# The last block of an attention-and-convolution kernel worked in two parts, with three small reorderings before it

## The chip, the cores and the metric

The kernel runs on one core of a Trainium2 chip. The time is that of the device in microseconds (us), for one execution of the whole program; the median over several executions is compared. The engines are TensorE (PE, with its weight loads as PEld), VectorE (DVE), ScalarE (ACT), GpSimd (POOL) and SyncE (SP); SP, ACT and POOL also issue transfers (DMA).

## The reference

Two layers act on x of shape 8 x 64 x 64 x 64 (batch, channels, height, width), all in four-byte floats. The first is attention over the 4096 pixels of an image, with the means of queries and keys taken off, and a unary term:

```python
sim = softmax(einsum('bcn,bcm->bnm', q - q_mean, k - k_mean) / 8, axis=2)
out = einsum('bnm,bcm->bcn', sim, v) + out_unary[:, :, None]
x = x + out.reshape(b, C, h, w)
```

The second takes the signs of the result, convolves them with signed weights of 1x1, 3x3 and 5x5 taps, scales each and adds the three, and gates the sum by the image's mean:

```python
s = qconv_bn(x, w1) + qconv_bn(x, w3) + qconv_bn(x, w5)   # binact(x) = sign(x), bin_weight(w)
gate = sigmoid(grouped(mean(s, axis=(2, 3)), gw) + gb)     # then a channel shuffle
return s * gate[:, :, None, None] + x
```

`bin_weight` takes the sign of each weight less its output channel's mean, times the mean of the absolute values. The gate needs the whole image's s, so nothing of an image can be stored before its last row of s is there.

## The kernel before, in words

Two images share the 128 partitions: a pair. There are four pairs. A pair's 4096 queries are worked in eight blocks of `QB` = 512, so there are 32 blocks, numbered g from 0 to 31. A block is a loop of `NK` = 32 steps over tiles of 128 keys. In a step, `scores` (L493) makes four 64x64 matmuls, one in each quadrant of the array, into a score bank `ps` and ScalarE takes the exponential of 128x1024 into a tile `e` (a pool of five buffers, L508); `weighted` (L511) makes four matmuls from the previous step's `e` into two accumulators `acc` (L516); `summed` (L524) lets VectorE add `e` to a running sum `es` (L534). Four-byte matmuls are recorded as two instructions each. In all blocks but the last, four of the 32 tiles are added in DRAM by transfers instead (`DRAM_TILES`).

What else has to be done is hung onto the steps by `plan(g)` (L1092): `put(i, f)` calls f after step i's matmuls were issued. This list alone sets the order on every engine; there is no scheduler behind it. At step 0 of block g, `weighted_out` (L536) copies the two accumulators of block g−1 to SBUF, the first by ScalarE (L541), the second by VectorE (L542), then `mix_rows` (L990) makes the queries of block g+1 and the convolutions of block g−3, as products of combined rows: `products(k, names)` of the 5x5 and the 3x3. Those of the 3x3 go to the two banks of the accumulators (0 to 3 to the first, 4 and 5 to the second). `hold` (L827) takes a product out scaled, by ScalarE, and `join` (L836) adds another on VectorE. In the steps that follow, the sums of block g−1 come back (`fold_first`, `fold`, `fold_last`, `spread`), the values are tested for 0 and infinity (`check_block`), and `added`, `finish`, `signs_wide` and `signs` make x and its signs.

In block 1, `mean_rows_out` (L219) makes the weights' means by one product (`nmb_p`, L221) and a copy, `centre` (L226) takes them from the weights on VectorE, and `weight_signs` (L232) takes the signs on ScalarE (L233), for the 5x5, the 3x3 and the 1x1 at steps 3 to 10.

In the last block (g = 31) there is no next block. `mix` (L939) makes the plain convolutions of block 29 at step 22 and of the first six rows of the joint blocks 30 and 31 at step 27; a 5x5 or 3x3 tap is one matmul (L891), and `convs_out` (L899) adds the three results on VectorE (L915). After the loop, block 31 is finished: accumulators out in parts of 320 and 192 columns, sums by a matmul with ones (`sums_wide`, L598), reciprocals in pieces of 128 (L609), `added`, `finish`, signs, copies of signs to the other half of the partitions by VectorE and GpSimd, then `mix` for rows 6 to 10 and 11 to 15, the test, `gate_mean` and `gate` (L919 to L932), and the stores: two blocks by a product with the gate on a diagonal (L1261) and ScalarE, six by VectorE (L936) and SyncE (L937).

Of the kernel before, what the change touches and what calls it, by code (L numbers as in the profile page):

```python
# [40 lines left out]
DRAM_TILES = (5, 11, 17, 23)  # L41
LOW, HIGH = 1e-20, 1e20
# [3 lines left out]
def conv_seq_kernel(ctx, tc, x, wq, wk, wv, vecs, w1, w3, w5, wtap, gw, out):  # L46
# [72 lines left out]
    fit = cp.tile([P, 2, n_pairs * (NQ + 1)], F32, tag="fit", name="fit")  # L119
# [157 lines left out]
    class Pair:  # L277
# [3 lines left out]
        def __init__(self, name, xt):  # L281
            self.name, self.x = name, xt
            self.xs = sm.tile([P, 8], F32, tag="xs", name=f"xs_{name}")
            self.q, self.x2, self.s, self.y1, self.acc = {}, {}, {}, {}, {}
            self.es, self.r, self.joint, self.sc, self.gap, self.t = {}, {}, None, None, None, None
# [147 lines left out]
        def check(self, r, i, sides=(0, 1)):  # L433

            w = r.shape[-1]
            for side in sides:
                if w < QB:
                    junk = self.tile(sm, "ck", f"{i}_{side}", (P, 8), BF16)
                else:
                    junk = self.tile(fp, "rc", f"ck_{i}_{side}", dtype=BF16)  # L440
                nc.scalar.activation(  # L441
                    junk[:, 0:w],
                    r,
                    AF.Sign,
                    bias=lim[:, side : side + 1],
                    scale=1.0 - 2.0 * side,
                    accum_out=fit[:, side, i : i + 1],
                )
# [44 lines left out]
        def scores(self, qb, j, neg=None):  # L493
            ps = ps_s.tile([P, 2, QB], F32, tag="s", name=f"ps_{self.name}_{qb}_{j}")
            for h in range(2):
                for b in range(2):
                    nc.tensor.matmul(  # L497
                        ps[img[h], b, :],
                        self.x[img[b], bass.ds(j * P + h * H, H)],
                        self.q[qb][img[b], :],  # L500
                        start=True,
                        stop=neg is None,
                    )
# [3 lines left out]
            e = ep.tile([P, 2, QB], F32, tag="e", name=f"e_{self.name}_{qb}_{j}")  # L507
            nc.scalar.activation(e, ps, AF.Exp, scale=1.0 / 8.0)  # L508
            return e

        def weighted(self, qb, j, e):  # L511
            if j == 0:
                self.acc[qb] = acc_banks(f"acc_{self.name}_{qb}")
            for b in range(2):
                for h in range(2):
                    nc.tensor.matmul(  # L516
                        self.acc[qb][h][img[b], :],
                        self.v[img[h], j, img[b]],
                        e[img[h], b, :],
                        start=(j == 0),  # L520
                        stop=(j == NK - 1),
                    )

        def summed(self, qb, j, e, dram=False):  # L524
# [5 lines left out]
            elif j == 1:  # L530
                self.es[qb] = self.tile(sm, "es", qb, (P, 2, QB))
# [4 lines left out]
        def weighted_out(self, qb, parts=(slice(0, QB),)):  # L536

            acc = self.acc[qb]
            self.acc[qb] = [self.tile(fp, f"o{h}", qb) for h in range(2)]
            for c in parts:  # L540
                nc.scalar.copy(self.acc[qb][0][:, c], acc[0][:, c])  # L541
                nc.vector.tensor_copy(self.acc[qb][1][:, c], acc[1][:, c])  # L542
# [55 lines left out]
        def sums_wide(self, qb):  # L598
            self.sums_p = m_tile(f"su_{self.name}_{qb}")
            es = self.es.pop(qb)  # L600
            for b in range(2):
                nc.tensor.matmul(self.sums_p[img[b], :], ones[:, 0:C], es[:, b, :], start=True, stop=True)  # L602

        def reciprocals_wide(self, qb, cols):
            if cols.start == 0:
                self.r[qb] = self.tile(fp, "r", qb)
            for a in range(cols.start, cols.stop, P):
                c = slice(a, min(a + P, cols.stop))
                nc.vector.reciprocal(self.r[qb][:, c], self.sums_p[:, c])  # L609

        def added(self, qb, cols=slice(0, QB)):
            if cols.start == 0:
                self.x2[qb] = self.tile(bp, "x2", qb)
            acc = self.acc[qb]
            nc.vector.tensor_tensor(self.x2[qb][:, cols], acc[0][:, cols], acc[1][:, cols], ALU.add)
# [211 lines left out]
        def hold(self, z, i, n, by):  # L827
# [6 lines left out]
            nc.scalar.activation(out, z, AF.Identity, scale=frac[:, by : by + 1])  # L834
# [64 lines left out]
        def convs_out(self, rows, z, n):  # L899
# [10 lines left out]
            if n == 0:  # L910
                nc.scalar.activation(s, z[0][0][:, 0:w], AF.Identity, bias=shift, scale=scale[:, 0:1])
                return
            for h in range(len(z[n])):
                gap = dict(accum_out=self.gap_column()) if (n, h) == (2, 1) else {}
                nc.vector.scalar_tensor_tensor(  # L915
                    s, z[n][h][:, 0:w], scale[:, n : n + 1], s, ALU.mult, ALU.add, **gap
                )

        def gate_mean(self):  # L919
            self.ga = self.tile(sm, "ga", 0, (P, 1))  # L920
            nc.vector.tensor_reduce(self.ga, self.gap[:, 0 : self.n_gaps], AX.X, ALU.add)

        def gate(self):
            pg = m_tile(f"pg_{self.name}")
            for b in range(2):
                nc.tensor.matmul(
                    pg[img[b], 0:1], gw_s[img[b], img[b]], self.ga[img[b]], start=True, stop=True
                )
            self.gt = self.tile(sm, "gt", 0, (P, 1))
            nc.scalar.activation(self.gt, pg[:, 0:1], AF.Exp, bias=ngb, scale=-1.0 / N)  # L930
# [8 lines left out]
    def mix(q, c, one=None, two=None):  # L939
# [47 lines left out]
        if c is not None:  # L987
            p.convs_out(rows, z, 2)

    def mix_rows(q, c):  # L990
# [6 lines left out]
        if c is not None:  # L997
# [6 lines left out]
            seqs[0] += products(5, 4, 5) + products(3, 4, 5, 0, 1, 2, 3) + [((1,), 0, 1.0)]  # L1004
# [13 lines left out]
        for _, h, b, (n, i, _) in order:  # L1018
# [27 lines left out]
            elif n == (3, 5):  # L1046
                p.hold(acc[1][:, 0 : 4 * HH], 6, 2, 0)
# [34 lines left out]
    def attend(pairs):  # L1082
# [9 lines left out]
        def plan(g):  # L1092
# [32 lines left out]
            if g == 1:  # L1125
                put(0, mean_rows_out)
# [9 lines left out]
            if g >= 1:  # L1136
# [6 lines left out]
                put(13, p.added, b)  # L1143
                put(15, p.finish, b)
                put(16, p.signs_wide, b, 2)
                put(18, p.signs_wide, b, 1)
                put(20, p.signs, b)
# [27 lines left out]
            if g == 1:  # L1175
                for i, n in enumerate((2, 1, 0)):
                    put(3 + 3 * i, centre, n)
                    put(4 + 3 * i, weight_signs, n)
# [27 lines left out]
            if g == n_blocks - 1:  # L1206
                put(1, pairs[-1].join_blocks)
                put(22, lambda: mix(None, rows(n_blocks - 3), one_bank, score_banks))
                put(27, lambda: mix(None, (pairs[-1], pairs[-1].joint_rows(0, 6)), one_bank, score_banks))
            return at  # L1210

        for g in range(n_blocks):
            pr, qb = divmod(g, NQ)
            at = plan(g)
            p = pairs[pr]
            for j in range(NK):
                new = (p, qb, j, p.scores(qb, j))
                if pending is not None:
                    pending[0].weighted(*pending[1:])
                    pending[0].summed(*pending[1:], g < n_blocks - 1)  # L1220
                for f, a in at.pop(j, ()):
# [3 lines left out]
        pending[0].weighted(*pending[1:])  # L1225
        pending[0].summed(*pending[1:])
# [3 lines left out]
        parts = [(0, 5), (5, ROWS)]  # L1230
        p.weighted_out(b, [slice(r0 * HH, r1 * HH) for r0, r1 in parts])
        p.sums_wide(b)

        pre = acc_banks("pre")
        for i in range(2):
            nc.tensor.matmul(pre[i], ident, p.x2[i], start=True, stop=False)
        warm(10)
        halves = [slice(r0 * HH, r1 * HH) for r0, r1 in parts]
        p.added(b, halves[0])
        p.reciprocals_wide(b, halves[0])  # L1240
        p.finish(b, halves[0])
        p.added(b, halves[1])
        p.reciprocals_wide(b, slice(halves[1].start, halves[1].start + P))
        for (r0, r1), cols in zip(parts, halves):
            if r0 > 0:
                p.reciprocals_wide(b, slice(cols.start + P, cols.stop))
                p.finish(b, cols)
            for n in (2, 1):
                p.signs_wide(b, n, r0, r1, None)
                p.copy_signs(b, n, r0, r1, (nc.vector.tensor_copy, nc.gpsimd.tensor_copy))  # L1250
            p.signs(b, r0, r1, nc.gpsimd.tensor_copy)
        mix(None, (p, p.joint_rows(6, 11)), one_bank, score_banks)
        mix(None, (p, p.joint_rows(11, 16)), one_bank, score_banks)
        p.check(p.r[b], n_blocks - 1)
        p.gate_mean()
        p.gate()
        diag_g = sm.tile([P, P], F32, tag="diag_g", bufs=1, name="diag_g")
        nc.vector.tensor_scalar(diag_g, ident, p.gt, None, ALU.mult)
        rows_p = rows_of(n_pairs - 1)
        for i in range(2):  # L1260
            nc.tensor.matmul(pre[i], diag_g, p.s[i], start=False, stop=True)  # L1261
            nc.scalar.copy(p.s[i], pre[i])
            nc.scalar.dma_start(out=of[rows_p, bass.ts(i, QB)], in_=p.s[i])
        for i in range(2, NQ):
            p.store(i, rows_p)

    with tc.manual_schedule():
# [21 lines left out]
        attend([first] + [None] * (n_pairs - 1))  # L1289


    nb_ = sm.tile([P, 1], F32, tag="nb", name="nb")
    nc.vector.tensor_reduce(nb_, fit, AX.XY, ALU.add)
    nc.vector.tensor_scalar(nb_, nb_, n_pairs * (16.0 * NQ + 2.0) - 16.0 + 2 * QB, None, ALU.is_equal)
    pb = m_tile("pb")
    nc.tensor.matmul(pb[:, 0:1], ones, nb_, start=True, stop=True)
    good = sm.tile([P, 1], I32, tag="good", name="good")
    nc.vector.tensor_copy(good, pb[:, 0:1])
# [121 lines left out]
```

## Time and profile before

| what | value |
|---|---|
| time, median of 3 | 1902.15 us (1902.07 to 1902.22) |
| the profiled execution: its own time | 1902.25 us |
| its span, first to last instruction | 1900.4 us |
| busy: TensorE, VectorE, ScalarE | 1881.3, 1587.7, 1276.6 us |
| granted TensorE clock, mean | 0.997 |
| one `e` of 128x1024: exponential, sum | 1025 ns, 1221 ns |
| last store issued, last one landed | 1893.1, 1897.9 us |

The busy shares come from matmuls whose ends are modelled, so TensorE's 99% says that it is seldom without work, not how well it is used. In a timeline row the first two numbers are start and length in us, then come engine, line, operation, output<-input, and in brackets the idle time before it and what ended it. In the chain of waits each row is a stretch of the chain that ended last: start, length, engine and line.

### The profile page before, as it was taken

To read this page: it belongs to the slowest core of one execution; us is meant where nothing else is said; L and a number is where in the kernel's file an instruction comes from. 1 tells how busy PE (TensorE), PEld (TensorE's weight loads), DVE (VectorE), ACT (ScalarE), POOL (GpSimd) and SP (SyncE) were. 2 spreads that over 40 slices of the span, in tenths; PEclk is the share of its full clock that TensorE was granted. 3 is DMA by queue.
4 is the path that set the end of the run, shared out by engine and by line. 5 is a ranking of instruction groups with operands and counts; after the bars stand their busy time and mean duration, and the time that the engine had idled before them with its cause. 6 is when DMAs were issued, how large, how long until landed. Compare 5 with 4: busy or idle time off the path is not lost.

```text
span 1900.4 us, 50311 instructions
## 1 busy us (share of the span) xinstructions
PE 1881.3 (99%) x21494; PEld 785.8 (41%) x21494; DVE 1587.7 (84%) x2485; ACT 1276.6 (67%) x1639; POOL 129.4 (7%) x177
## 2 busy tenths in 40 slices
PE   9999999999999999999999999999999999999997
PEld 4334344343344434444434444434433344444343
DVE  6888888889888888888888888888887888887876
ACT  5666776666666676666666667666666666666663
POOL 0000000000000000000000000000000000000000
PEclk9999999999999999999999999999999999999998
DMA  4334433333333533333333444333333344333311
GB/s 124 60 62 106 83 65 72 66 58 72 67 70 87 117 83 80 65 72 66 58 71 68 104 111 92 52 78 67 70 67 66 63 85 93 85 71 63 72 35 47
DMA packets 73025, 142.23 MB, mean 75 GB/s; under 512 B 10380, under 2 KB 40920, under 8 KB 72664
## 3 DMA queue, kind: packets, MB, share of 16 engines
q0 software_dynamic: 22352, 81.29, 24.1%
q1 hardware_dynamic: 49864, 56.53, 10.3%
q8 instruction: 170, 2.79, 0.6%
q10 hardware_dynamic: 576, 1.11, 0.2%
q14 instruction: 63, 0.52, 0.1%
HBM read 39.27 MB, written 89.78 MB: 68 GB/s over the span
## 4 chain that ended last, share of the span: by engine, by line
PE 90%; DVE 1%; DMA 0%; ACT 0%; issue 0%; ACTq 0%
PE ps L497 43%; PE acc L516 43%; PE z L804 2%; PE pq L483 1%; PE pv L336 1%; PE z L891 0%; PE z_5e L804 0%; DMA es<-e 0%; PE pre L1261 0%; DVE r L609 0%; ACT e L508 0%; ACT rc_ck L441 0%; DVE es L534 0%; PE su L602 0%; DVE es_j L915 0%
## 5 line engine op out<-in xcount | busy, mean ns | idle before, releaser
L508 ACT ACTIVATE e<-ps 128x1024 f32<-128x1024 f32 x1024 | 1049.0, 1025 | 571.9 <-PE ps L497 557.7
L534 DVE TENSOR_TENSOR es<-es,e 128x1024 f32<-128x1024 f32 x836 | 1020.5, 1221 | 192.4 <-ACT e L508 178.7
L497 PE MATMUL ps<-q,x 64*64 64x512 f32 x8192 | 1087.3, 590 | 1.5 <-ACT q L466 0.8
L516 PE MATMUL acc<-e,v 64*64 64x512 f32 x8192 | 1085.2, 589 | 0.6 <-ACT e L508 0.6
L516 PEld LDWEIGHTS acc<-e,v 64*64 64x64 f32 x8192 | 326.3, 131 | 554.8 <-ACT e L508 316.6
L497 PEld LDWEIGHTS ps<-q,x 64*64 64x64 f32 x8192 | 348.2, 133 | 489.8 <-issue 264.3
L555 POOL DMA_DIRECT2D es<-e x93 | 80.1, 862 | 900.3 <-ACT e L508 597.3
L871 DVE SCALAR_TENSOR_TENSOR sb<-pt,sb 128x256 f32<-128x256 f32 x174 | 65.8, 419 | 0.0
L804 PEld LDWEIGHTS <-wc 64*64 64x64 bf16 x3364 | 60.0, 106 | 2.7 <-issue 1.0
L555 POOL DMA_DIRECT2D es<-es x31 | 26.6, 859 | 440.2 <-DVE es L534 426.1
L532 DVE TENSOR_TENSOR es<-e,e 128x1024 f32<-128x1024 f32 x32 | 39.2, 1225 | 18.1 <-ACT e L508 18.1
L804 PE MATMUL z<-ec,wc 64*64 64x128 bf16 x1392 | 53.6, 217 | 0.0
L804 PE MATMUL z<-t,wc 64*64 64x128 bf16 x1392 | 53.1, 217 | 0.3 <-DVE o L542 0.3
L652 ACT ACTIVATE s<-x,vec 128x512 bf16<-128x512 f32 (+2 forms) x66 | 46.1, 702 | 5.6 <-DVE x L620 5.6
L834 ACT ACTIVATE pt<-z,frac 128x256 f32<-128x256 f32 (+1 forms) x87 | 41.1, 543 | 8.9 <-PE z L804 8.9
L839 DVE SCALAR_TENSOR_TENSOR pt<-z_5e,frac,pt 128x256 f32<-128x256 f32 x29 | 14.0, 484 | 38.2 <-PE z_5e L804 38.2
L553 POOL DMA_DIRECT2D es<-e x31 | 17.4, 561 | 340.2 <-ACT e L508 328.9
L542 DVE COPY o<-acc 128x512 f32<-128x512 f32 (+2 forms) x33 | 22.2, 675 | 9.6 <-PE acc L516 9.6
L845 DVE TENSOR_TENSOR pt<-pt 128x384 f32<-128x384 f32 x58 | 29.6, 552 | 0.0
L336 PEld LDWEIGHTS pv<-wx,x 64*64 64x64 f32 x1024 | 22.1, 134 | 16.6 <-issue 8.9
L570 DVE TENSOR_TENSOR e_parts<-e_parts 128x512 f32<-128x512 f32 x31 | 21.3, 687 | 7.3 <-DMA e_parts<-es 7.3
L620 DVE SCALAR_TENSOR_TENSOR x<-x,ou,x 128x512 f32<-128x512 f32 (+2 forms) x33 | 24.3, 736 | 1.2
(178 smaller groups left out, 880.5 us busy)
## 6 DMA issues: line engine op xcount, KB each, us to landing
es<-e POOLq DMA_DIRECT2D x124, 512.0 KB, 5.3
es<-es POOLq DMA_DIRECT2D x31, 512.0 KB, 5.4
e_parts<-es SPq DMA_DIRECT2D x124, 128.0 KB, 3.1
r<-rc SPq DMA_DIRECT2D x62, 128.0 KB, 2.8
out<-sb SPq DMA_DIRECT2D x28, 256.0 KB, 3.0
x<-in_x SPq DMA_DIRECT2D x24, 256.0 KB, 4.9
ec<-t SPq DMA_DIRECT2D x29, 99.0 KB, 4.8
xc<-in_x SPq DMA_DIRECT2D x30, 72.0 KB
```

What stands on the lines that cost most here:

```text
L336: nc.tensor.matmul(pv[img[h], b, i * w : (i + 1) * w], self.x[img[b], bass.ds((4 * g + i) * P + h * H, H)], self.wx[img[b], :], start=True ...
L497: nc.tensor.matmul(ps[img[h], b, :], self.x[img[b], bass.ds(j * P + h * H, H)], self.q[qb][img[b], :], start=True, stop=neg is None,)
L508: nc.scalar.activation(e, ps, AF.Exp, scale=1.0 / 8.0)
L516: nc.tensor.matmul(self.acc[qb][h][img[b], :], self.v[img[h], j, img[b]], e[img[h], b, :], start=(j == 0), stop=(j == NK - 1),)
L532: nc.vector.tensor_tensor(self.es[qb], self.first, e, ALU.add)
L534: nc.vector.tensor_tensor(self.es[qb], self.es[qb], e, ALU.add)
L555: nc.gpsimd.dma_start(out=out, in_=e, accum_op=ALU.add)
L652: nc.scalar.activation(sy[n][0][:, rows, pad : pad + HH], self.x2[qb][:, r0 * HH : r1 * HH].rearrange("p (h w) -> p h w", w=HH), AF.Sign, ...
L804: nc.tensor.matmul(z[img[b], :].rearrange("p (q w) -> p q w", w=HH), wc[k][img[h], n, c * C : c * C + C], src[:, first : first + step + 1 ...
L834: nc.scalar.activation(out, z, AF.Identity, scale=frac[:, by : by + 1])
L845: nc.vector.tensor_tensor(self.pairs[:, :, :, r, :], t[:, 0:3, 0], t[:, 0:3, 1], op)
L871: nc.vector.scalar_tensor_tensor(out, x, by, out, ALU.mult, ALU.add, **gap)
```

## The change

There are four parts.

In `mix_rows`, the products of the 3x3 come in the order 0, 4, 5, 1, 2, 3 instead of 4, 5, 0, 1, 2, 3, and product 5 is taken out of its bank by VectorE instead of ScalarE.

In block 1, `mean_rows_out` moves from step 0 to step 5, `centre` from steps 3, 6, 9 to 7, 10, 13, and `weight_signs` from 4, 7, 10 to 8, 11, 14.

The last block is worked in `PARTS`: 384 queries in 32 steps with one tile of 128 keys each, then 128 queries in eight steps with four tiles of keys each. The steps of its plan are scaled by 512/384 (`plan_last`), `added` to `signs` start two steps sooner, and all of the first part's finish (sums, reciprocals, signs and their copies by transfers, test) is hung onto the second part's steps.

After the loop only 128 queries are left to finish. The convolutions are cut at rows 6 to 11 and 12 to 15, with other banks; the mean covers all but the last rows, and the logits add the last two columns of sums by further matmuls (`gate_logits`); of the last rows, one 5x5 result is scaled by ScalarE and added late. The product with the gate's diagonal is kept for one block, the diagonal is made by ScalarE, and VectorE and SyncE store seven blocks. The final test for 0 and infinity moves into this stretch.

```diff
+PARTS = ((slice(0, 384), 1), (slice(384, QB), 4))
-        def scores(self, qb, j, neg=None):
+        def scores(self, qb, j, neg=None, part=(slice(0, QB), 1)):
+            cols, n = part
+            w = cols.stop - cols.start
...
+            for i in range(n):
+                for h in range(2):
+                    for b in range(2):
+                        nc.tensor.matmul(
+                            ps[img[h], b, i * w : (i + 1) * w],
+                            self.x[img[b], bass.ds((n * j + i) * P + h * H, H)],
+                            self.q[qb][img[b], cols],
...
+            for t in range(n * j, n * j + n):
+                at = (t - n * j) * w
+                for b in range(2):
+                    for h in range(2):
+                        nc.tensor.matmul(
+                            self.acc[qb][h][img[b], 0:w],
+                            self.v[img[h], t, img[b]],
+                            e[img[h], b, at : at + w],
...
+            if vector:
+                nc.vector.tensor_scalar(out, z, frac[:, by : by + 1], None, ALU.mult)
+            else:
+                nc.scalar.activation(out, z, AF.Identity, scale=frac[:, by : by + 1])
...
-            seqs[0] += products(5, 4, 5) + products(3, 4, 5, 0, 1, 2, 3) + [((1,), 0, 1.0)]
+            seqs[0] += products(5, 4, 5) + products(3, 0, 4, 5, 1, 2, 3) + [((1,), 0, 1.0)]
...
-                p.hold(acc[1][:, 0 : 4 * HH], 6, 2, 0)
+                p.hold(acc[1][:, 0 : 4 * HH], 6, 2, 0, True)
...
-                put(0, mean_rows_out)
+                put(5, mean_rows_out)
...
-                    put(3 + 3 * i, centre, n)
-                    put(4 + 3 * i, weight_signs, n)
+                    put(7 + 3 * i, centre, n)
+                    put(8 + 3 * i, weight_signs, n)
...
+        def plan_last():
+            at, (first, _) = {}, PARTS
+            for i, steps in plan(n_blocks - 1).items():
+                at[i * QB // first[0].stop] = steps
...
+            put(NK - 5, lambda: mix(None, rows(n_blocks - 3), one_bank, score_banks))
+            put(NK - 2, lambda: mix(None, (p, p.joint_rows(0, 6)), one_bank, score_banks))
+            put(NK, p.weighted_out, b, cols)
+            put(NK + 1, p.added, b, cols)
+            put(NK + 1, p.sums_wide, b, first)
+            put(NK + 1, p.reciprocals_wide, b, cols)
+            put(NK + 2, p.finish, b, cols)
+            put(NK + 3, lambda: p.check(p.r[b][:, cols], n_blocks - 1))
+            put(NK + 4, p.signs_wide, b, 2, 0, r1)
+            put(NK + 5, p.signs_wide, b, 1, 0, r1)
+            put(NK + 6, p.signs, b, 0, r1)
...
+        mix(None, (p, p.joint_rows(6, 12)), acc_bank(0), score_banks)
         p.gate_mean()
-        p.gate()
+        p.check(p.r[b][:, cols], n_pairs * (NQ + 1))
+        mix(None, (p, p.joint_rows(12, 16)), acc_bank(1), score_banks, True)
+        p.gate_logits()
...
+        nc.tensor.matmul(pre, ident, p.x2[0], start=True, stop=False)
+        p.gate_out()
+        nc.scalar.activation(diag_g, ident, AF.Identity, scale=p.gt)
+        nc.tensor.matmul(pre, diag_g, p.s[0], start=False, stop=True)
+        nc.scalar.copy(p.s[0], pre)
+        nc.scalar.dma_start(out=of[rows_p, bass.ts(0, QB)], in_=p.s[0])
+        p.store(1, rows_p)
...
         for i in range(2, NQ):
             p.store(i, rows_p)
```

## The prediction

> **What bounds the kernel now.** I read the page's busy shares first, then the chain of waits, then the timeline of four places: a block boundary, block 1, the value products, the end.
>
> ```profile
> PE 1881.3 (99%) x21494; PEld 785.8 (41%) x21494; DVE 1587.7 (84%) x2485; ACT 1276.6 (67%) x1639; POOL 129.4 (7%) x177
> PE 90%; DVE 1%; DMA 0%; ACT 0%; issue 0%; ACTq 0%
> ```
>
> TensorE sets the time. A step of the loop is `ps` 0.858 us, then `acc` 0.858 us, back to back; 32 steps make 54.9 us, 32 blocks 1758 us. Only a hole in TensorE, or the end, can be gained. At the boundary before block 30's second step:
>
> ```profile
> 1750.91 0.69 DVE L542 COPY o<-acc 128x512 f32<-128x512 f32 x1 [0.32 <-PE acc L516]
> 1750.94 0.58 ACT L541 COPY o<-acc 128x512 f32<-128x512 f32 x1
> ...
> 1751.53 0.22 PE L804 MATMUL z<-ec,wc 64*64 64x128 bf16 x1
> 1751.65 0.21 PE L804 MATMUL z<-t,wc 64*64 64x128 bf16 x1
> ```
>
> Products normally start 0.03 us apart at most here; this start comes 0.12 after the last, 0.05 after VectorE's copy has emptied the second accumulator at 1751.60: a hole of 0.09. ScalarE had emptied the first at 1751.52. Every boundary from block 3 to 30 shows the same. Block 1 has two larger holes:
>
> ```profile
> 76.60 0.44 DVE L490 TENSOR_SCALAR q<-pq,mx 128x224 f32<-128x224 f32 x1
> 77.10 0.59 PE L221 MATMUL nmb_p<-diag,ones 64*128 64x192 f32 x2 [1.37 <-DVE q L490]
> 85.76 1.54 ACT L233 ACTIVATE wt<-w_tap 128x1600 bf16<-128x1600 f32 x1
> 88.26 1.09 PE L516 MATMUL acc<-e,v 64*64 64x512 f32 x8 [0.28 <-ACT e L508]
> ```
>
> The weights' means wait for a bank that the queries hold, and all later matmuls wait behind them; then ScalarE's signs of 1600 columns make an exponential late (0.45 lost: `acc` was due at 87.81). The chain at the end, from the last exponential:
>
> ```profile
> 1869.85 1.03 ACT e L508
> 1870.91 1.24 DVE es L534
> 1872.19 1.10 PE su L602 x4
> 1873.32 2.19 DVE r L609 x3
> ...
> 1876.88 0.87 DVE r L609
> ...
> 1881.49 0.96 PE z L891 x16
> ...
> 1885.59 0.57 DVE es_j L915 x2
> ...
> 1887.38 0.17 DVE gt L932
> ```
>
> From TensorE's last `acc` (ends 1871.8) to the gate (1887.56) take 15.8 us, serial, with VectorE's reciprocals (0.73 per 128 columns), then signs, copies and two convolutions.
>
> **What the Trainium skill says.** "PSUM — Partial Sum Buffer", PSUM bank collisions raise a hardware error: guard PSUM by bank and quadrant, so a product may not enter an accumulator that is still being read; the hole of 0.09 is that. The same page, Engine vs sequencer instructions: ScalarE's and VectorE's queues are strict FIFO; the late exponential of block 1 agrees. "TensorE: Matmul & The Clock Gate", LDWEIGHTS: about P/1.2 ns for P columns, and Part 3, The mechanism: loads overlap only when the row group differs. That makes 53 ns per 64 columns and, two in turn, an estimate of 107 ns for four quadrants. The value products, four-byte with 65 moving columns, contradict it:
>
> ```profile
> 29.05 0.64 PE L336 MATMUL pv<-wx,x 64*64 64x65 f32 x32
> 29.51 1.09 PE L497 MATMUL ps<-q,x 64*64 64x512 f32 x8
> ```
>
> 32 matmuls with their loads pass in 0.46 us, 0.0575 per four. The trace decides.
>
> **3x3's products.** Product 0 needs the accumulator that ScalarE empties 0.07 to 0.08 sooner. Products 4 and 5 follow three columns (0.17) later, when VectorE is done. 29 boundaries by 0.07: −2.0 us; at least 0 (the hole reappears), at most 29 by 0.09, 2.6. The evacuation of product 5 moves from ScalarE (0.45, 256 columns) to VectorE (0.47, by L490's 0.44 for 224). VectorE is idle there 1.3 us before the join that waits for `z_5e`, so it costs nothing; uncovered, 0.47 by 29 is 13.6.
>
> **Block 1.** The means' product leaves step 0. Queries end at 75.54, `ps` runs to 76.4, `acc` waits for VectorE's copy (76.00 to 76.68), and step 2's `ps` begins at 77.60 instead of 79.38: −1.78. In step 5 the product costs its own 0.32. Then it gets worse: VectorE's queue from the means' copy is copy 0.36, fold 0.68, 0.42, 0.45, one sum 1.23, 0.41, 0.20, 0.45, centring 1.81, together 6.0 us with no room between. With TensorE's step 5 at 83.2 the copy begins at 85.64, centring ends at 91.6, the signs end at 93.2, the exponential queued behind them at 94.1, while `acc` is due at 93.05: a hole of 1.15 for the old 0.45. Sum −1.78 + 0.32 + 0.70 = −0.8; between −1.9 (no new hole) and +0.3.
>
> **The last block.** Columns are the same, so TensorE's products cost the same, if the loads, doubled to 512 recorded, hide: four per 0.107 us of 128-column passes, against 0.0575 shown. The steps of 384 last 1.288; the sum of 768 columns is 0.95 (between L615's 0.686 for 512 and L534's 1.221 for 1024), 1.02 with the dependence on the one before; the exponential about 0.80. VectorE's slack per microsecond falls from 1 − 1.29/1.717 = 25% to 1 − 1.02/1.288 = 21%; over the 20 us of joins, folds and pairs that is 0.8 us. What TensorE gets added:
>
> - sums of the first 384 columns inside the loop, 0.86 × 0.75 = 0.65;
> - sign of block 30 at step 18, queued on ScalarE behind VectorE's `finish`, which now sits 1 us behind its exponential: exponentials 19 and 20 slip, 1.0 (0 to 2.5);
> - short first step, waiting for the accumulators: 0.1;
> - after each convolution the second-next `ps` takes the bank that VectorE empties; a shorter step gives 0.43 less cover, twice: 0.85 (before: 0.42 and 0.13 lost);
> - the first 128-column `acc` behind both evacuations: 0.3;
> - the two checks of 384 (0.8 each) ahead of an exponential: 0.3.
>
> Together +3.2 (0.7 to 6): the last `acc` ends at 1875.0 on the old clock. From there, with the durations of 128 columns set a little under the rows of 192 (0.36, 0.42, signs 0.40): last sum 0.35, sums by TensorE 1.0, hand-over 0.3, one reciprocal of 128 0.73, two products 0.75, three signs 0.85, z0's evacuation 0.65: at +4.6 VectorE starts on the convolution. The convolution of rows 6 to 11 needs only the first part's signs and runs on TensorE meanwhile (2.8 us); rows 12 to 15 follow (1.87) and are done 0.8 before VectorE's end. GpSimd's copies of 128 columns (0.35 for 192 now) lie beside rows 6 to 11; uncovered they would cost 0.7. VectorE: three sums of 384 (0.62 each, 2.1 with gaps), mean 0.2, two of 256 (0.48, 0.57), to +7.95; logits 0.35, exponential 0.26, two small ones 0.31, latencies 0.45: gate at +9.3, not +15.8. The late addition (0.42) and the test of the limits (0.23, 0.15) that stand on VectorE before the gate's last steps fit beside logits and exponential (0.9 with hand-overs); without that cover they cost 0.8. So −6.4 + 3.2 = −3.2.
>
> After the gate VectorE stores seven blocks instead of six but no longer makes `diag_g` first; the last issue is at gate + 5.7 against 5.6, and the transfers' landing (1897.9, 10.3 after the gate) moves with it: 0 ± 0.8. SyncE issues one store more (0.36 to 0.6), in that count; its new part copies (four transfers of the first part) have 3 us before the convolution asks.
>
> **Sum.** −2.0 − 0.8 − 3.2 = −6.0 against the profiled execution's 1902.25 us (span 1900.4 and 1.85 around it; the median is 1902.15): **1896.2 us**, 0.3% less. A measurement of this kernel can tell about 0.2% (3.8 us) from no change.
>
> **Rivals.** (1) Loads bound the second part. The loads of four quadrants span 0.16 us where they are recorded in a group; if 128 such groups take that instead of 0.107, +6.8: 1903.0, slower than before. It decides from 0.154 per group on; two full loads of 0.131 in turn would give +19.8 and 1916. Against it: the value products at 0.0575. (2) VectorE falls behind in the first part by more than the four to five `e` buffers cover (3 to 4 us): +3, 1899.2. For it: VectorE is busy without a break from 1812 to 1834 already. Against: it had caught up by 1834.6. (3) The first product meets the same hole, or VectorE's evacuation is late: no gain at the boundaries, 1898.2. For it: ScalarE is only 0.07 ahead. (4) The signs' wait and block 1's new hole don't arise: 1894.0.
>
> **From this to numbers.** Forecast 0.60, rivals 0.05, 0.15, 0.10, 0.10. The forecast's own range is 1894.6 to 1898.0. 1893.5 to 1900.0 holds rivals 2 to 4 as well and leaves 2 in 10 out. Faster by over 0.2% (below 1898.35): forecast, rival 4, half of 3, some of 2: 0.80; within 0.2%: 0.17; slower: 0.03.
>
> **What would show it.** Boundary holes of 0.02 before the first 3x3 product; in block 1 `nmb_p` with no wait of a microsecond and one hole over 1 us beside the signs of 1600 columns; in the last block a hole of about 1 us at step 19; 128-column `ps` groups of 16 matmuls (32 recorded) in 0.86 us; the gate about 9.3 after the last `acc`, in one reciprocal of 128. Wrong would be: those groups over 1 us; exponentials waiting for VectorE's sums through the first part; sums of 768 columns slower than 0.95; transfers that hold the stores back beyond gate + 10.3.

## The result and the profile after

The changed kernel takes 1895.65 us (median of 7 runs, 1895.03 to 1895.74), the kernel before 1902.07 (7 runs, 1901.16 to 1902.64): ratio 0.9966, 95% interval 0.9956 to 0.9976. That is 6.4 us less. Run again later beside other kernels, the unaltered changed kernel gave 1896.42 against 1902.16, ratio 0.9970 (0.9959 to 0.9981), 5.7 us less. The forecast was 1896.2, 6.0 less.

The page of the kernel after has TensorE's share and the chain hardly altered:

```profile
PE 1875.8 (99%) x22006; PEld 796.7 (42%) x22006; DVE 1602.7 (85%) x2519; ACT 1266.4 (67%) x1624; POOL 127.6 (7%) x174
PE 88%; DVE 2%; DMA 1%; issue 0%; ACT 0%; SPq 0%; DVEq 0%; ACTq 0%
```

TensorE's busy time fell by 5.5 us. Behind the last `acc` alone it has 5.7 less, 10.1 in place of 15.8, since the tail has less work: ten products whose result nobody reads went with the change, and half of those that add the gated sum to x. The timeline of the kernel before has the ten in the wait for the signs, off the chain of waits:

```profile
1875.02 2.40 PE L155 MATMUL warm<-ones 128*128 128x128 f32 x20
```

What leaving them out alone does was not tried; the mean clock granted over the tail's convolutions is 1.00 in both kernels. With ends that are modelled, part of a wait counts as busy too. So the comparison goes by starts. The table takes them from the timelines, in us: the first score product of the program; from the first score product of block 1 to that of its step 12; from step 20 of block 2 to step 1 of block 31; from there to the last start of an `acc`; to the end of the gate; to the end of the span.

| profiled execution | first score | block 1 | blocks 2 to 30 | last block | to the gate | to the end |
|---|---|---|---|---|---|---|
| before | 13.38 | 24.41 | 1642.83 | 61.40 | 16.12 | 12.84 |
| after | 12.69 | 23.90 | 1640.28 | 65.57 | 9.40 | 11.86 |
| after, again | 13.02 | 23.90 | 1640.26 | 65.58 | 9.41 | 13.00 |
| order and hold alone | 12.61 | 24.41 | 1640.60 | 61.34 | 16.12 | 12.35 |
| block 1 alone | 12.65 | 23.90 | 1643.29 | 61.39 | 16.12 | 12.98 |
| last block alone | 12.92 | 24.41 | 1642.71 | 65.88 | 9.41 | 12.48 |
| hold on ScalarE | 13.22 | 23.90 | 1644.42 | 66.02 | 9.41 | 13.03 |
| signs in four | 13.08 | 22.89 | 1640.26 | 65.57 | 9.40 | 12.53 |
| sign later | 13.11 | 23.89 | 1640.38 | 64.78 | 9.39 | 12.50 |
| all mended | 12.85 | 22.89 | 1640.30 | 64.87 | 9.41 | 12.59 |

The four columns in the middle repeat to within 0.1 us from one kernel to the next where nothing was changed, but for the cases told below. The first and the last don't: the first score waits for the input's first transfer and stands anywhere from 12.6 to 13.4, and the last transfers land 11.9 to 13.0 after the gate. The spans of the first two rows differ by 7.1 us; 0.7 of that is the start and 1.0 the end, and neither is the change.

The column of blocks 2 to 30 takes in step 0 of block 31, so with the last block's change it is some 0.3 shorter. Two stretches are left out: block 0, and step 12 of block 1 to step 20 of block 2. The first three rows agree there to 0.2, but three rows (last block alone, signs in four, sign later) have block 0 longer by 1.0 to 1.1, though nothing was changed in it.

At block 30's boundary (timeline of the kernel after) the products now run through the end of ScalarE's copy at 1748.38 and that of VectorE's at 1748.45, 0.05 apart at most, where 0.12 stood:

```profile
1747.76 0.69 DVE L553 COPY o<-acc 128x512 f32<-128x512 f32 x1 [0.32 <-PE acc L527]
1747.80 0.58 ACT L552 COPY o<-acc 128x512 f32<-128x512 f32 x1
...
1748.38 0.22 PE L826 MATMUL z<-t,wc 64*64 64x128 bf16 x1
1748.39 0.22 PE L826 MATMUL z<-ec,wc 64*64 64x128 bf16 x1
1748.43 0.21 PE L826 MATMUL z<-t,wc 64*64 64x128 bf16 x1
```

Block 1, timeline of the kernel after: the means' product without a wait, VectorE's centring up to 91.4, the signs, and behind them the exponential for which `acc` waits (due at 92.96, 0.97 lost):

```profile
84.62 0.59 PE L223 MATMUL nmb_p<-diag,ones 64*128 64x192 f32 x2
...
89.61 1.78 DVE L230 TENSOR_TENSOR w_tap<-w_tap,nmb 128x1600 f32<-128x1600 f32 x1
91.42 1.54 ACT L235 ACTIVATE wt<-w_tap 128x1600 bf16<-128x1600 f32 x1 [0.67 <-DVE w_tap L230]
92.87 1.01 ACT L515 ACTIVATE e<-ps 128x1024 f32<-128x1024 f32 x1
93.93 1.09 PE L527 MATMUL acc<-e,v 64*64 64x512 f32 x8 [0.83 <-ACT e L515]
```

In the last block, here ScalarE's timeline at step 18, the sign waits for VectorE's last product of `finish` and two exponentials stand behind it. TensorE's next `acc` comes 1.38 after its `ps` (1831.33 to 1832.71), where 0.645 is the rule: 0.74 lost.

```profile
1831.23 0.72 ACT L674 ACTIVATE s<-x,vec 128x512 bf16<-128x512 f32 x1 [0.79 <-DVE x L642]
1831.86 1.49 ACT L515 ACTIVATE e<-ps 128x768 f32<-128x768 f32 x2
```

The end of the kernel after in the chain of waits (start, length, engine and line). The last `acc` starts at 1872.01, the gate is there at 1881.42:

```profile
1860.14 2.58 DVE r L631 x3
...
1871.47 1.23 DVE es L545
1872.75 1.12 PE su L616 x16
1873.89 0.97 DVE r L631
...
1875.60 0.70 ACT s L674 x2
1876.30 0.29 ACT cl_j L668
1876.58 0.57 ACT es_j L936
1877.17 0.63 DVE es_j L948
...
1880.40 0.42 DVE es_j L952
...
1881.25 0.17 DVE gt L981
```

One reciprocal of 128 columns stands on the chain where four stood, one of these of 64, and three additions of 384 and two of 256 columns. New is the first row: from 1860.14 on, the chain of this kernel runs over VectorE. The three reciprocals of the first part put its sums about 3.5 us behind (the first could have begun at 1859.24 and begins at 1862.72), and it works them off one after the other until the last, which is 0.35 late.

### The profile page after: what moved, and what is told of

Same layout as the page of the kernel before. It is cut to its first block, busy times and chain, and to the rows that moved or that the text cites. A ratio compares the mean times of both kernels' runs of the same rounds, so it can differ in the third digit from the quotient of the medians.

```text
span 1893.3 us, 51371 instructions
## 1 busy us (share of the span) xinstructions
PE 1875.8 (99%) x22006; PEld 796.7 (42%) x22006; DVE 1602.7 (85%) x2519; ACT 1266.4 (67%) x1624; POOL 127.6 (7%) x174
## 4 chain that ended last, share of the span: by engine, by line
PE 88%; DVE 2%; DMA 1%; issue 0%; ACT 0%; SPq 0%; DVEq 0%; ACTq 0%
PE ps L504 42%; PE acc L527 42%; PE z L826 2%; DVE es L545 1%; PE pv L338 1%; PE pq L485 1%; PE z L916 0%; DMA es<-e 0%; PE z_5e L826 0%; DVE es_j L948 0%; DVE r L631 0%; DMA e_parts<-es 0%; DVE sb L985 0%; PE su L616 0%; ACT e L515 0%
## 5 line engine op out<-in xcount | busy, mean ns | idle before, releaser
L515 ACT ACTIVATE e<-ps 128x1024 f32<-128x1024 f32 (+1 forms) x1032 | 1049.2, 1017 | 571.1 <-PE ps L504 558.1
L545 DVE TENSOR_TENSOR es<-es,e 128x1024 f32<-128x1024 f32 (+1 forms) x842 | 1018.7, 1210 | 191.2 <-ACT e L515 176.8
L504 PE MATMUL ps<-q,x 64*64 64x512 f32 (+2 forms) x8448 | 1090.1, 577 | 2.1 <-ACT q L468 0.8
L527 PE MATMUL acc<-e,v 64*64 64x512 f32 (+2 forms) x8448 | 1088.3, 577 | 1.9 <-ACT e L515 1.9
L527 PEld LDWEIGHTS acc<-e,v 64*64 64x64 f32 x8448 | 334.2, 131 | 549.0 <-ACT e L515 315.7
L504 PEld LDWEIGHTS ps<-q,x 64*64 64x64 f32 x8448 | 356.5, 133 | 485.3 <-issue 263.3
L543 DVE TENSOR_TENSOR es<-e,e 128x1024 f32<-128x1024 f32 (+1 forms) x33 | 40.0, 1214 | 16.8 <-ACT e L515 16.8
L859 ACT ACTIVATE pt<-z,frac 128x256 f32<-128x256 f32 (+1 forms) x58 | 30.6, 577 | 17.0 <-PE z L826 17.0
L346 ACT COPY v<-pv 128x512 f32<-128x512 f32 x32 | 18.7, 586 | 8.7 <-PE pv L338 8.7
```

What stands on the lines that cost most here:

```text
L504: nc.tensor.matmul(ps[img[h], b, i * w : (i + 1) * w], self.x[img[b], bass.ds((n * j + i) * P + h * H, H)], self.q[qb][img[b], cols], star ...
L515: nc.scalar.activation(e, ps[:, :, 0 : n * w], AF.Exp, scale=1.0 / 8.0)
L527: nc.tensor.matmul(self.acc[qb][h][img[b], 0:w], self.v[img[h], t, img[b]], e[img[h], b, at : at + w], start=(t == 0), stop=(t == NK - 1),)
L543: nc.vector.tensor_tensor(self.es[qb], self.first, e, ALU.add)
L545: nc.vector.tensor_tensor(self.es[qb], self.es[qb], e, ALU.add)
```

## The experiments

**One part at a time.** Three kernels with one part of the change each.

*Order and hold alone*: the kernel before with

```diff
-products(3, 4, 5, 0, 1, 2, 3)
+products(3, 0, 4, 5, 1, 2, 3)
...
-p.hold(acc[1][:, 0 : 4 * HH], 6, 2, 0)
+p.hold(acc[1][:, 0 : 4 * HH], 6, 2, 0, True)
```

> The kernel before with the first part of the change alone: the order 0, 4, 5, 1, 2, 3 and product 5 taken out by VectorE. Theory (the hole at each boundary is the wait for VectorE's copy, and the three columns in front cover it): hole 0.02 or less, 0.08 gained at each of 29 boundaries and some more at block 31, 2.3 to 2.5 us less than before, 1899.7. Rival (most of the gain lies in the last block, the boundaries give it back elsewhere): within 0.5 us of before.

Measured: 1899.46 (13 runs) against 1901.96 (48 runs), ratio 0.9988 (0.9980 to 0.9996): 2.5 less. The trace has 0.07 to 0.08 less at each boundary from block 3 on, 2.23 over blocks 2 to 30. The theory holds.

*Block 1 alone*: the kernel before with

```diff
-put(0, mean_rows_out)
+put(5, mean_rows_out)
...
-put(3 + 3 * i, centre, n)
-put(4 + 3 * i, weight_signs, n)
+put(7 + 3 * i, centre, n)
+put(8 + 3 * i, weight_signs, n)
```

> The kernel before with the weights' means, centring and signs later in block 1, nothing else. Theory from the two traces: the wait for the bank goes (1.7 gained net), the product costs 0.6 in step 5, the hole by the signs of 1600 columns grows from 0.45 to 1.0: 0.5 us less than before at the end of block 1, 1901.6. The forecast's own sum was 0.8. Rival: the later signs push something else in blocks 1 and 2, and the end is within 0.2 us of before or later.

Measured: 1902.02 (13 runs) against 1901.96, ratio 1.0000 (0.9992 to 1.0008). The trace has the 0.51 in block 1 as expected, and loses 0.46 later: at the boundaries of blocks 19 and 25 VectorE's addition of the 5x5's end rows begins 0.40 after the semaphore that it waited for (1117.29 to 1117.69), elsewhere 0.06, and TensorE's next score product waits for the bank. The profile shows nothing that VectorE did in those 0.40. The kernel with the hold on ScalarE has the same late beginning at the same two boundaries and loses about 0.1 at each; the changed kernel and the last block alone do not have it. The cause stays open; so does whether it comes in every execution. What is shown is that this part is worth half a microsecond in block 1 and nothing that 13 runs can see.

*The last block alone*: the changed kernel with both edits above undone.

> The changed kernel with the order of the 3x3 and block 1 as they were: the last block in two parts alone. Theory (the parts are independent): from the first score of block 31 to the end 3.5 us less than before, 1898.5, and with the other two parts 6.3 together. Forecast: 3.2 less. Rival (the parts need each other, or the profile of the changed kernel, whose first score stood 0.7 earlier, was a lucky one): 2.8 or less.

Measured: 1899.04 (20 runs) against 1901.96, ratio 0.9984 (0.9977 to 0.9991): 2.9 less, between the forecast's 3.2 and the rival's 2.8. The last block is 0.3 longer here than in the changed kernel (65.88 against 65.57), and also in the next kernel (66.02): the two in which ScalarE takes product 5 out. So the parts lean on each other a little. The three alone come to 2.5 − 0.1 + 2.9 = 5.3, the whole to 6.4 and 5.7.

**The hold that was costed at nothing.**

```diff
-p.hold(acc[1][:, 0 : 4 * HH], 6, 2, 0, True)
+p.hold(acc[1][:, 0 : 4 * HH], 6, 2, 0)
```

> The changed kernel with product 5 taken out by ScalarE again. Theory (there is room on either engine between product 5 and the join that needs it): same time within 0.3 us. Rival (0.45 of ScalarE ahead of an exponential at each boundary makes it late, or on VectorE it is what makes room): 0.1 to 0.4 us at each of 29 boundaries, 3 to 12 us more.

Measured: 1900.42 (12 runs) against 1901.96, ratio 0.9990 (0.9982 to 0.9999). It gives back over 4 of the 6 us. Over blocks 2 to 30 the trace has 1644.42 against 1640.28: 4.1 more, 0.14 to 0.16 between the score products of steps 1 and 2 at the boundaries from block 3 on, 0.20 at two of them. The timeline at block 30's boundary shows where:

```profile
1753.53 1.42 ACT L859 ACTIVATE pt<-z,frac 128x256 f32<-128x256 f32 x3 [0.39 <-PE z L826]
1754.03 1.06 PE L504 MATMUL ps<-q,x 64*64 64x512 f32 x8
...
1754.99 1.09 PE L527 MATMUL acc<-e,v 64*64 64x512 f32 x8
```

ScalarE takes three products out in a row, done at 1754.95. The last of them is the first accumulator, and the new block's first `acc` needs it: it starts at 1754.99, 0.96 after the score product in place of 0.86. The old order had the same three evacuations 0.17 earlier and just fitted. In the changed kernel there are two:

```profile
1749.35 1.05 ACT L859 ACTIVATE pt<-z,frac 128x256 f32<-128x256 f32 x2 [0.57 <-PE z L826]
```

They end at 1750.40, `acc` starts at 1750.52. The order alone thus loses some 0.14 a block to gain 0.08; the rival was right, and the move to VectorE is what makes the order pay. What that move does in the old order was not run.

**Block 1's signs in pieces.**

```diff
+for a, z in cut:
+    nc.scalar.activation(wt[:, a:z, :], w_tap[:, a:z, :], AF.Sign)
...
-put(8 + 3 * i, weight_signs, n)
+cut = [10, 16, 22, 29, 35] if n == 2 else [FIRST[n], FIRST[n + 1]]
+for k in range(len(cut) - 1):
+    put(8 + 3 * i + k + (n < 2), weight_signs, cut[k : k + 2])
```

> The changed kernel with block 1's signs of 1600 columns cut in four of 384 to 448, one a step at steps 8 to 11, the 3x3's one step later. Theory (the hole of 0.97 before an acc at 92.06 to 93.93 is the exponential queued behind 1.54 us of signs, and a piece of 0.5 fits beside an exponential of 1.02 in a step of 1.72): the hole goes, 0.9 to 1.0 less at the end of block 1. Rival (the hole is VectorE's: sums, fold and centring leave it late): the hole stays within 0.3.

Measured: 1894.80 (5 runs) against 1902.07, ratio 0.9964 (0.9950 to 0.9978); block 1 takes 22.89 in place of 23.90. ScalarE's timeline:

```profile
92.96 0.52 ACT L236 ACTIVATE wt<-w_tap 128x384 bf16<-128x384 f32 x1 [0.67 <-DVE w_tap L230]
93.39 1.01 ACT L514 ACTIVATE e<-ps 128x1024 f32<-128x1024 f32 x1
```

The piece still waits for the centring, but the exponential is only 0.5 behind it, and `acc` starts on time at 94.45. The hole was ScalarE's queue.

**The last block's sign one step later.**

```diff
-put(at0 + 3, p.signs_wide, b, 2)
-put(at0 + 5, p.signs_wide, b, 1)
+put(at0 + 3 + (at0 < 13), p.signs_wide, b, 2)
+put(at0 + 5 + (at0 < 13), p.signs_wide, b, 1)
```

> The changed kernel with the first two signs of block 30 one planned step later in the last block (steps 20 and 22 in place of 18 and 21). Theory (the sign waits on ScalarE for VectorE's last product of finish and holds an exponential up): the hole of 0.74 at step 19 of the last block goes, and 0.5 to 0.75 less at the first convolution after it; the two signs in steps that lie closer give back at most 0.2. Rival (the sum of VectorE's work is too much there, and another exponential waits for an e buffer in place of it): 0.2 or less.

Measured: 1895.69 (5 runs) against 1902.07, ratio 0.9965 (0.9951 to 0.9979). The last block takes 64.78 in place of 65.57: the 0.74 and a little more. By the time alone it could not be told from no change; the stage shows it.

**The banks after a convolution.** In the changed kernel the score product two after the first convolution inside the last block starts 1.50 after its `acc` in place of 0.645, and 1.21 after the second. The experiment lets ScalarE take out one of the two 5x5 results, as the kernel's last convolution does.

```diff
-mix(None, rows(n_blocks - 3), one_bank, score_banks)
+mix(None, rows(n_blocks - 3), one_bank, score_banks, True)
-mix(None, (p, p.joint_rows(0, 6)), one_bank, score_banks)
+mix(None, (p, p.joint_rows(0, 6)), one_bank, score_banks, True)
```

> The changed kernel with the two convolutions inside the last block taken out as the last one is: one of the two 5x5 results by ScalarE into a tile beside, added by VectorE afterwards. Theory (the score product two after a convolution waits for the bank that VectorE empties last): the holes of 0.85 and 0.56 shrink to 0.2 and 0.1, about 1.1 less at the end of the loop; VectorE has two additions more (0.7 and 0.6), which its slack there takes up or not: 0.3 given back at most. Rival (ScalarE's 0.8 and 0.7 stand ahead of the next exponential, and acc waits in place of ps): 0.3 or less.

Measured: 1896.38 (7 runs) against 1902.07, ratio 0.9971 (0.9960 to 0.9983); the last block takes 65.82, 0.25 more. The starts are 1.43 and 1.19 apart: hardly less. VectorE's addition waits for ScalarE's evacuation, here at the first convolution:

```profile
1848.53 0.75 DVE L948 SCALAR_TENSOR_TENSOR sb<-z,scale,sb 128x512 f32<-128x512 f32 x1 [1.72 <-ACT vu_late L944]
```

The second try takes the sum of the image from VectorE's last addition alone (the two convolutions pass `late` as 2):

```diff
-gap = dict(accum_out=self.gap_column()) if n == 2 and (late or h == 1) else {}
+gap = dict(accum_out=self.gap_column()) if n == 2 and (late is True or h == 1 and not late) else {}
...
-if side is not None:
+if side is not None and late is True:
     nc.vector.tensor_tensor(s, s, side, ALU.add)
+elif side is not None:
+    nc.vector.scalar_tensor_tensor(s, side, 1.0, s, ALU.mult, ALU.add, accum_out=self.gap_column())
```

> As conv_side, but the image's sum is taken by the last of VectorE's additions alone, and ScalarE's takes none: in conv_side VectorE's 5x5 addition began at 1848.53, after ScalarE's 0.69 and the read of its accumulator had ended at 1848.49, though its bank was full from 1847.7. Theory (the two wait for each other over the tile of sums, not for the banks): VectorE starts at once, the score product two after the convolution no longer waits, the holes of 0.85 and 0.56 fall to 0.2 and 0.1, and the last acc ends 0.9 to 1.1 earlier than in the changed kernel. Rival (VectorE's extra addition is then late for the sums, as the 0.4 lost ahead of the sums' product in conv_side): 0.5 or less.

Measured: 1895.83 (5 runs) against 1902.16, ratio 0.9966 (0.9953 to 0.9979); the last block takes 65.66, 0.09 more. The sum's tile was only a part of it:

```profile
1847.45 0.75 DVE L948 SCALAR_TENSOR_TENSOR sb<-z,scale,sb 128x512 f32<-128x512 f32 x1 [1.63 <-ACT vu_late L944]
...
1848.26 0.88 PE L504 MATMUL ps<-q,x 64*64 64x384 f32 x8 [0.28 <-DVE sb L948]
```

VectorE starts when ScalarE has ended (1847.42) again: in the trace its addition waits for a semaphore that ScalarE sets at 1847.43. ScalarE's instruction read the other half of the same two-bank tile; that the shared tile is why the program has this wait is likely, not shown. So the two evacuations still run one after the other, and the starts are 1.33 and 1.09 apart. What that saves, 0.3, goes at the end of the part: VectorE's copy of the second accumulator ends 0.3 later after block 31's start than in the changed kernel, and the next `acc` has none of the gain left. That the score product waits for VectorE's evacuation is shown; that it could be had for nothing is not. Two separate tiles weren't tried.

**Do weight loads bound the second part?** Each score product of the second part in two of 64 columns:

```diff
+d = w // 2 if n > 1 else w
-for i in range(n):
+for i, c in [(i, c) for i in range(n) for c in range(0, w, d)]:
-    ps[img[h], b, i * w : (i + 1) * w],
+    ps[img[h], b, i * w + c : i * w + c + d],
-    self.q[qb][img[b], cols],
+    self.q[qb][img[b], cols.start + c : cols.start + c + d],
```

> The changed kernel with each score product of the second part cut in two of 64 columns: twice the products and twice the weight loads for the same columns, in eight groups; acc as it was. Theory of the forecast (four loads pass in 0.0575, so four products of 64 columns, 0.0537, are just bound by them): a ps group takes 0.92 in place of 0.87, 0.4 us in all. Rival (a group of four loads takes 0.107, the estimate from the price by columns): 1.7 a group, 6.7 us more in all. Rival (0.16): 2.6 a group, 13.6 more.

Measured: 1901.49 (one run) against 1902.07. The groups without a pause take 0.93 to 0.98 us, 0.058 to 0.061 per four products with their loads: the forecast's price, and far from the rival's 0.107. But the last block takes 71.61 in place of 65.57, because TensorE stands still inside groups. Its groups by form, and two rows of its timeline:

```profile
L528 PE MATMUL acc<-e,v 64*64 64x128 f32 x256 | 9.7, 272 | 2.0 <-issue 1.8 <-ACT e L516 0.2
L505 PE MATMUL ps<-q,x 64*64 64x64 f32 x512 | 9.6, 220 | 2.7 <-issue 2.5 <-DVE es_j L949 0.2
```

```profile
1867.99 0.70 PE L505 MATMUL ps<-q,x 64*64 64x64 f32 x33 [1.52 <-issue]
1871.46 0.21 PE L505 MATMUL ps<-q,x 64*64 64x64 f32 x1 [0.97 <-issue]
```

"issue" is time in which it waited for nothing that the profile shows. In the record of transfers, packets of 16 KB on an instruction queue had landed at 1858.86, 1866.48, 1870.18 and 1873.93; TensorE went on after its four longest pauses at 1860.23, 1867.99, 1871.46 and 1875.20. To part the number of instructions from the size of the products, only two of the eight groups were cut:

```diff
-d = w // 2 if n > 1 else w
+d = w // 2 if n > 1 and j in (2, 5) else w
```

> As half_columns, but only the third and the sixth of the eight score products of the second part are cut in pieces of 64 columns. In half_columns TensorE stood still 1.74, 1.19, 1.11 and 0.87 us inside groups with nothing in the profile to wait for, and each of the first three ended 1.3 to 1.5 us after a 16 KB packet of the instruction queue had landed, one packet in 3.8 us. Theory (TensorE is short of instructions, 128 a group in place of 64 for eight groups on end, and the pauses are that): single groups take 0.92 to 0.98 with no pause over 0.3, the last acc within 0.4 us of the changed kernel's 65.6 after the second score product. Rival (the loads themselves stall in groups so small): each of the two groups holds a pause of 0.5 or more.

Measured: 1897.26 (one run) against 1901.67; the last block 67.19. Both expectations missed. The first cut group takes 0.98 without a pause; the second holds one; and another stands in a group that was not cut:

```profile
1867.54 0.21 PE L505 MATMUL ps<-q,x 64*64 64x64 f32 x1 [0.64 <-issue]
...
1871.84 0.27 PE L505 MATMUL ps<-q,x 64*64 64x128 f32 x1 [0.57 <-issue]
```

The second row is of 128 columns, and two of the four long pauses before stand in `acc` groups of 128 columns, so small products are not needed for a pause. Again they end 1.3 and 1.5 after a packet had landed (1866.23, 1870.34). That TensorE was short of instructions fits all six pauses. The record lets it be estimated: in the changed kernel 174 such packets land, with 256 products and loads of TensorE recorded between two in the median. In the second part with halved columns they land 3.6 to 3.9 us apart, which makes 66 to 71 instructions a us by this estimate. A halved group of scores and its `acc` group, without a pause, have 192 in some 1.8 us, 107 a us; the changed kernel has 64 in 0.87 us, 73 a us. It was not shown directly, since no record names the wait. Shown is that the changed kernel has no such pause, and that 64 instructions more in two of its groups are enough for two.

**The mended kernel.** Signs in four, the sign later and the second form of the convolutions' sums together, beside the changed kernel itself.

> Signs in four, signs one step later and the convolutions' sums as in conv_side_one_sum together. Theory (three holes in different places add up): 1.0 + 0.75 + 0.9 = 2.6 less than the changed kernel measured beside it, about 1893.0. Rival (what one gives another takes, at the end of the first part where VectorE has the least slack): 1.8 or less.

> The changed kernel unaltered, as the mark for the run beside it. Its first profile began 0.7 earlier than that of before. Theory (that is the first transfer of the input, another in each execution): 1895.65 within 0.4, and a first score anywhere between 12.6 and 13.4 us. Rival (the change itself starts sooner): first score again at 12.7.

Measured: 1894.55 (5 runs, 1893.83 to 1895.50) against 1896.42 for the changed kernel (7 runs, 1895.86 to 1897.28) and 1902.16 for the kernel before; ratio to before 0.9961 (0.9947 to 0.9974). It is 1.9 less than the changed kernel, near the rival's 1.8: the stages have 1.01 less in block 1 and 0.71 in the last block, and the convolutions' sums add nothing (at the last `acc`, 0.09 of the sign's 0.79 is lost). The changed kernel's first score stood at 13.02 this time, so the earlier start is not the change's.

## Why the prediction was right, and where it was not

- **3x3's products**, −2.0 forecast: 2.23 in the trace of that part alone, 2.5 by its median. The reason, the wait for VectorE's copy, is the one that fell away. The hold moved to VectorE did cost nothing, but the step judged it by itself. It asked what VectorE would lose and took ScalarE's side as free, while with the new order ScalarE's third evacuation would have held up the first `acc`, 4.1 in all.
- **Block 1**, −0.8 forecast: −0.51 in the trace. The wait removed gave 1.73 net for 1.78. The signs' hole is 0.97, for 1.15, and cost 0.60 more than the old one, for 0.70. The mis-sized term is the product in step 5: 0.63 in place of 0.32.
- **The last block on TensorE**, +3.2 forecast for the end of the last `acc`: +3.5. The table's column has +4.17, but it goes to the last start, which stands 0.36 before the end of a group of 512 columns and 0.04 before that of a group of 128, so 0.32 of it belongs to the tail. Another 0.21 is saved before step 1 by the shorter first score product, and 0.11 more at the boundary. By terms: sums inside the loop 0.80 for 0.65; the sign 0.79 (what moving it gave back) for 1.0; convolutions' banks 0.87 for 0.85; the short first step 0.3 for 0.1; the first 128-column products behind the evacuations 0.44 for 0.3; the tests for 0 and infinity 0.18 for 0.3. Loads, forecast to hide, cost 0.2: 16 groups of 0.873 in place of 0.858. The terms sum to 3.6. The short first step and the loads were sized too small.
- **The tail**, 6.4 less by the forecast: 6.4 less from the end of the last `acc` (15.8 before, 9.4 after). Inside it two errors cancel, which is luck. VectorE began the convolution's additions at +5.1 for +4.6, since the last sum was late and the reciprocal lasted 0.97 for 0.73. That 0.73 was misread: the three reciprocals of the prediction's 2.19 have 128, 128 and 64 columns, and the 0.87 in the same lines is one of 128. The rest was shorter than forecast.
- **After the gate**, 0 ± 0.8: within the scatter of 11.9 to 13.0 that kernels with the same end show.
- **Rivals.** Loads as the bound: refuted at 0.87 a group, and by 0.061 per four where they were forced. VectorE behind the buffers of `e`: in the first part TensorE ran its steps at 0.645 without a break but for the sign; it is VectorE that carries the chain afterwards, with 0.3 of delay at the last sum. In the kernel with two halved groups that sum begins 0.03 after its exponential in place of 0.35, and the gate comes 9.10 after the last start of `acc` in place of 9.40. No gain at the boundaries: didn't come, and the hold on ScalarE is the version of it that would have. No sign wait and no new hole in block 1: both came.

The errors had both signs and were small: 0.2 more gained at the boundaries, 0.3 less in block 1, 0.3 more lost in the last block. The total is nearer than its terms because they cancel. The stages sum to −2.2 − 0.5 + 3.5 − 6.4 = −5.6, to set beside 6.4 and 5.7 measured.

## What to carry to other kernels

When an edit moves work from one engine to another and another edit changes its time, cost the two together: ask what the old engine would do in the new order, not only whether the new one has room. Cut work that is queued ahead of a bound engine's supplier into pieces that fit between two of its deliveries, or put it where its input is already there; each such hole was worth 0.8 to 1.0 us here and cost a few lines. Read changes of this size by stages between fixed points of the trace, since start and end alone differ by a microsecond from one execution to the next.

## What was not expected of the hardware

- TensorE paused 0.8 to 1.7 us from one start to the next, with nothing in the profile to wait for, when some groups were cut in twice as many instructions; three of the six pauses stand in groups of 128 columns. Each of the six ended 1.3 to 1.5 us after a 16 KB packet on an instruction queue had landed.
- Quadrants of the array can run apart. In block 1 the changed kernel's first `acc` could start only on the accumulator that ScalarE had emptied by 75.26; the other came free at 75.99. One product began at 75.61, the other three at 76.03 and later. For 3.5 us the timeline shows `ps` and `acc` starts interleaved, one quadrant 0.43 to 0.49 ahead: its score product of step 2 starts at 76.46, before three products of the `acc` ahead of it in the program (76.53), and 2.2 earlier than before. The others start at 76.96, which on the clock of the kernel before is within 0.1 of the forecast's 77.60. The next product over the whole array (`po`, at 80.49) came after all of them, and step 3 took 0.49 longer than before. Of 2.2 us, 1.7 stayed.
- Two engines that evacuated two halves of one two-bank tile did so one after the other in both tries: VectorE began 0.03 us after ScalarE's end at each of the four convolutions. This is a wait in the program, not the hardware's own.
